# Attention and large-kernel convolution on one core: first statistics blocks ahead of ScalarE's square root, zeros of a mixed operand by GpSimd, first taps of layer 1 loaded in eight pieces

## The chip, the cores and the metric

The kernel runs on one core of one Trainium2 chip. A time is the device time of a whole launch in microseconds (us). A core has five engines, each with its own instruction queue, worked off in order: TensorE (PE, matmuls), VectorE (DVE), ScalarE (ACT), GpSimd (POOL) and SyncE (SP, which only issues DMAs here). DMAs are issued from SP, ACT and POOL; in the profile their queues are q1, q10 and q0.

## The reference, cut to what matters

The input x is 384 channels of 192 by 192 in float32. Each of two layers normalizes its input over 32 groups of channels, computes something from it, and adds the result to its input.

```python
# layer 0: a 1x1 convolution to q, k, v; 2x2 max pooling; a 3x3 depthwise convolution;
# attention over channels in 8 heads of 48 (4 top-k softmaxes, weighted); gelu; repeat 2x2; a 1x1 projection
x = x + _L0_conv_ref(_gn(x), w_qkv, b_qkv, w_dw, b_dw, w_proj, b_proj, temperature, a1, a2, a3, a4)
# layer 1: seven depthwise convolutions (13x13, 5x5, 7x7, 5x5 dilated 2, 3x3 dilated 3, 4, 5),
# each with its batch norm, summed
x = x + _L1_conv_ref(_gn(x), w0, ..., w6, bn0, ..., bn6)
```

```python
def _gn(v, G=32, eps=1e-5):
    g = v.reshape(B_, G, C_ // G, H_, W_)
    m = jnp.mean(g, axis=(2, 3, 4), keepdims=True)
    s = jnp.var(g, axis=(2, 3, 4), keepdims=True)
    return ((g - m) / jnp.sqrt(s + eps)).reshape(v.shape)
```

## The kernel before

The 384 channels are three blocks of 128 partitions (NJ = 3). The work goes through these stages, one after another.

**Statistics of x.** VectorE reads all of x once with bn_stats. The first 16 rows of the image come as four tiles `xt` (1152 KB each, all three channel blocks), which stay in memory and are used again in the next stage. The rest comes as 66 blocks `xs` (one channel block, 1536 columns, 768 KB), with ten tiles in rotation. `load_block` issues the DMA of a block: the first six and all odd ones from ScalarE, the other even ones from SP. VectorE takes the blocks in order, and `rows_stats` takes one xt tile ahead of blocks 0, 1, 3 and 5. On ScalarE, the table load and the square root of the batch norms' variances (`rsqrt`, L85, whose input waits for the load of `bn`) stand ahead of the loads. On SP, the four xt loads and that of the projection weights `wqk` stand ahead of block 6. GpSimd builds the combined 13x13 filter `wf` from the seven filters. The three small parameters bq, wd and bdw of the next stage are loaded from ScalarE.

**q, k and v (L332, about half of the time).** The stage goes over the image in bands of 8 rows, first for q and k, then for v. TensorE multiplies, VectorE pools (L343) and applies the depthwise taps (L379), ScalarE does the rest. Meanwhile GpSimd writes 2x2 sums of the normalized x to memory (`sums`), and Toeplitz bands of the layer-1 filter are written to memory (`zd`). Attention's softmax is computed between the steps. v ends up in memory that stays, as a tile of 128 x 3 x 96 x 96.

**Attention times v (L723).** A loop over 24 groups of 4 pooled rows multiplies the block-diagonal attention matrix `bd` with v. A head crosses from one channel block into the next, so the middle block of outputs also needs part of channel blocks 0 and 2. These parts go together into a mixed operand: `mix` copies them with GpSimd into one of three tiles `hx`, and the weights that belong to them are copied with ScalarE into `bdx`. The other partitions of both must be zero. VectorE writes these zeros at the head of the stage, in program order behind its last depthwise taps. ScalarE applies gelu in place.

**Projection (L1037).** It goes over channel block (i, 3) and group (b, 24), 72 cells n in all. For each cell TensorE multiplies, ScalarE evicts with the bias into a tile `pjs` (three in rotation, L1045) and issues its store to memory (`pd`, L1055), and VectorE adds the matching `sums` (tile `smj`, L1024, loaded from SP four cells ahead) and takes layer 1's statistics (`cell`, L1052, L1053). Between the cells the statistics of a finished channel block are turned into scales (`derive`), and the first two of layer 1's 48 groups of channels are prepared: `load_rows` loads rows of x (`raw`) and of the stored projection (`up`), `load_taps` the taps (`wt`, from `zd`), both from GpSimd; `residual` adds them, `patch` puts a term into the taps, `normalize1` and `arrange` make the patch tile `xp`. All of this is placed by hand at given cells; generators in `running` go on by one step for each cell.

**Layer 1 (L966).** For each of 48 groups of 8 channels, five matmuls for each channel work on taps and patches; loads, residual, normalization and the output run ahead or behind by a group or two. Its memory for later groups comes from what the projection gives back.

The order inside these stages is the program's own (`manual_schedule`). The framework places waits on semaphores: a DMA from SP or ScalarE takes one of eight semaphores in turn and waits for the last one to use it, and GpSimd's DMAs do the same with eight of their own. A tile whose memory another tile held waits for the last user of that one.

Of the kernel before, what the change touches and what calls it, by code (L numbers as in the profile page):

```python
# [14 lines left out]
P = 128  # L15
# [38 lines left out]
def tile_attn_then_large_kernel_conv(ctx: ExitStack, tc: tile.TileContext, a: dict, out: bass.AP):  # L54
# [106 lines left out]
    with (  # L161
        tc.tile_pool(name="s1", bufs=1) as s1,
        tc.tile_pool(name="sx", bufs=10) as sx,
        tc.tile_pool(name="s_ps", bufs=2, space=PSUM) as s_ps,
        tc.manual_schedule(),
    ):

        for B in range(2):
            for sb in range(2):
                load(B, sb)  # L170
        FX = 2 * R * 2 * W
        FB = 1536
        NX = (HW - FX) // FB
        NS0 = 2 * 2 * 2
        stats = s1.tile([P, NJ, NS0 + NX * (FB // 512), 6], F32, name="stats")
        bn = s1.tile([P, NJ, 4, 7], F32, name="bn")
        nc.gpsimd.dma_start(
            out=bn.rearrange("p j q i -> p j (q i)"), in_=a["bn"].rearrange("(j p) s -> p j s", p=P)
        )
        wf = s1.tile([P, NJ, KX, K0], F32, name="wf")  # L180
        nc.gpsimd.memset(wf, 0.0)
        wbs = []
        for i, (k, _) in enumerate(((K0, 1),) + BRANCHES):
            wb = s1.tile([P, NJ, k, k], F32, name=f"wb{i}")
            nc.gpsimd.dma_start(
                out=wb.rearrange("p j a b -> p j (a b)"), in_=a[f"w{i}"].rearrange("(j p) s -> p j s", p=P)
            )
            wbs.append(wb)
        xss = []

        def load_block(n):
            j, b = divmod(n, NX)
            xt = sx.tile([P, FB], F32, name=f"xs_{n}", tag="xs")

            eng = nc.scalar if n < 6 or n % 2 == 1 else nc.sync
            eng.dma_start(out=xt, in_=x[j * P : (j + 1) * P, FX + b * FB : FX + (b + 1) * FB])
            xss.append(xt)

        scale = in_one(rsqrt(s1, bn[:, :, 3, :], 1e-5, "bn"))
        nc.vector.tensor_mul(scale, scale, bn[:, :, 0, :])  # L200
        sh = s1.tile([P, NJ, 7], F32, name="sh")
        nc.vector.tensor_mul(sh, bn[:, :, 2, :], scale)
        nc.vector.tensor_sub(sh, bn[:, :, 1, :], sh)
        nc.vector.tensor_reduce(shift, sh, AX.X, ALU.add)
        for n in range(10):
            load_block(n)
        c0 = BC - 1
        for j in range(NJ):
            nc.gpsimd.tensor_scalar(wf[:, j, c0 : c0 + K0, :], wbs[0][:, j], scale[:, j, 0:1], None, ALU.mult)
            for i, (k, r) in enumerate(BRANCHES):  # L210
                o = PAD - r * (k - 1) // 2
                n = r * (k - 1) + 1
                zv = wf[:, j, c0 + o : c0 + o + n : r, o : o + n : r]
                wb = wbs[i + 1][:, j]
                nc.gpsimd.tensor_scalar(wb, wb, scale[:, j, i + 1 : i + 2], None, ALU.mult)
                nc.gpsimd.tensor_add(zv, zv, wb)

        def rows_stats(n):
            xt = xts[n // 2, n % 2]
            for j in range(NJ):  # L220
                nc.vector.bn_stats(stats[:, j, 2 * n, :], xt[:, j, :512])
                nc.vector.bn_stats(stats[:, j, 2 * n + 1, :], xt[:, j, 512:])

        for n in range(NJ * NX):
            if n in (0, 1, 3, 5):
                rows_stats((n + 1) // 2)
            j, b = divmod(n, NX)
            xt = xss.pop(0)
            for q in range(FB // 512):
                nc.vector.bn_stats(stats[:, j, NS0 + b * (FB // 512) + q, :], xt[:, q * 512 : (q + 1) * 512])  # L230
            if n + 10 < NJ * NX:
                load_block(n + 10)
            if b == NX - 1:
                nc.vector.bn_aggr(mv0[:, j, :], stats[:, j].rearrange("p n s -> p (n s)"))  # L234
        nc.sync.dma_start(
            out=wfd.rearrange("(j p) s -> p j s", p=P), in_=wf.rearrange("p j x y -> p j (x y)")
        )
        nc.vector.tensor_copy(gn0, in_one(group_stats(s1, s_ps, mv0, "g0")))  # L238
# [7 lines left out]
    with ExitStack() as ctx_v:  # L246
# [433 lines left out]
        with (  # L680
# [22 lines left out]

            bdx = b1.tile([P, P], F32, name="bdx")
            with tc.manual_schedule():
                for t in [bdx] + hx:
                    nc.vector.memset(t, 0.0)
                nc.scalar.copy(bdx[P - LO :], bd[P - LO :, 0, P : 2 * P])
                nc.scalar.copy(bdx[:HI], bd[:HI, 2, P : 2 * P])
                sms = [load_sums(b) for b in range(2)]  # L710
                for b in range(2):
                    mix(b)
                for b in range(NBB):
                    if b + 2 < NBB:
                        mix(b + 2)
                    if b + 2 < NBB:
                        sms.append(load_sums(b + 2))
                    pss = {}
                    for i in (0, 2, 1):
                        ps = b1_ps.tile([P, NBK], F32, tag=f"av{i}", name="av")  # L720
                        js = AV_BLOCKS[i]
                        for j in js:
                            nc.tensor.matmul(  # L723
                                ps,
                                lhsT=bd[:, j, i * P : (i + 1) * P] if j < NJ else bdx,
                                rhs=v[:, j, b * RB : (b + 1) * RB, :].rearrange("p r w -> p (r w)")
                                if j < NJ
                                else hx[b % 3],
                                start=(j == js[0]),
                                stop=(j == js[-1]),  # L730
                            )
                        pss[i] = ps
                    for i in (0, 2, 1):
                        nc.scalar.activation(
                            v[:, i, b * RB : (b + 1) * RB, :].rearrange("p r w -> p (r w)"), pss[i], AF.Gelu
                        )
                    sm = sms.pop(0)
                    for j in range(NJ):
                        nc.vector.bn_stats(stats[:, j, b, :], sm[:, j])
# [162 lines left out]
                )  # L902
                yield

        def load_taps(k, eng=nc.sync):
            wt = taps[k] = rotate("wt", k, k, [P, CC, ZS], 3)
            j, kk = divmod(k, KK)
            eng.dma_start(out=wt, in_=zds[j][kk * CC : (kk + 1) * CC].rearrange("c p z -> p c z"))

        def patch(k):  # L910

# [101 lines left out]
        with (  # L1013
# [4 lines left out]
            with tc.manual_schedule():  # L1018
# [9 lines left out]
                for n in range(NJ * NBB):  # L1028
# [7 lines left out]
                    for j in range(NJ):  # L1036
# [4 lines left out]
                            start=(j == 0),  # L1041
                            stop=(j == NJ - 1),
                        )
                    pj = by.tile([P, 2, RB // 2, WS], F32, tag="pjs", name="pjs")
                    nc.scalar.activation(  # L1045
                        pj.rearrange("p y r w -> p r y w"),
                        ps.rearrange("p (r y w) -> p r y w", y=2, w=WS),
# [12 lines left out]
                        ),  # L1060
                        in_=pj.rearrange("p y r w -> p y (r w)"),
                    )
                    if n == NBB + 4:
                        running.append(load_rows(0, nc.gpsimd))
                    if n == NBB + 9:
                        load_taps(0, nc.gpsimd)
                    if n == NBB + 13:
                        running.append(residual(0, nc.vector, 3))
                    if n == NBB + 20:
                        assert not running  # L1070
# [24 lines left out]
    with (  # L1095
        tc.tile_pool(name="l2", bufs=1) as l2,
        tc.tile_pool(name="more", bufs=1) as more,
        tc.tile_pool(name="lo", bufs=2) as lo,
    ):
        pools["more"] = more  # L1100
        with tc.manual_schedule():
            load_taps(1)
            patches(l2, 1)
            all_of(load_rows(2))
            last = None
            for k in range(NK):
                if k + 3 < NK:
                    all_of(load_rows(k + 3))
                if k + 2 < NK:
                    load_taps(k + 2)  # L1110
                    all_of(residual(k + 2))
                co = lo.tile([P, CC, NT, NBQ], F32, tag="co", name=f"co_{k}")
                for c in range(CC):
                    convolve(k, c, co)
                    if c == CC - 2:
                        advance()
                    if c == 0:
                        if k + 1 < NK:
                            all_of(arrange(k + 1))
                            patch(k + 1)  # L1120
                        if last is not None:
                            finish(k - 1, last, lo)

                    n = c - (CC - 3 if k == 0 else 3)
                    if 0 <= n < 3 and k + 2 < NK:
                        normalize1(k + 2, n)
                last = co
            finish(NK - 1, last, lo, 2, (nc.sync, nc.scalar, nc.gpsimd, nc.sync))
# [50 lines left out]
```

## Time and profile before

| What | us |
|---|---|
| median of 3 runs | 3153.32 (3152.84 to 3154.92) |
| profiled execution | 3152.71 |
| its span in the trace | 3150.9 |
| PE busy | 2952.2 (94%) |
| DVE busy | 2506.1 (80%) |
| ACT busy | 1229.4 (39%) |
| POOL busy | 896.7 (28%) |

The span is what the trace covers; 1.8 us of the profiled execution lie around it. Times inside the trace are counted from the span's start. In it, the statistics end at 158, attention times v begins at 1950, the projection at 2053 and layer 1 at 2214. A busy share is an average over all stages and says nothing about who sets the pace in one of them; for that the chain of waits is used, which goes back from the last instruction from each step to what released it.

### The profile page before, as it was taken

How to read it: one execution, taken by the hardware profiler on the slowest of the kernel's cores; microseconds unless marked ns; L12 is line 12 of the kernel's file. 1: busy time of each engine (PE TensorE's matmuls, PEld its weight loads, DVE VectorE, ACT ScalarE, POOL GpSimd, SP SyncE). 2: the span in 40 equal slices, each digit the busy share in tenths (PEclk: the TensorE clock that was granted, in tenths of full speed). 3: DMA queues.
4: the chain of work that ended last, by engine and by line, in shares of the span. 5: the costliest groups of instructions: out<-in, count | busy, mean ns of one | idle time of the engine just before them, and what ended most of it. 6: DMA issues, size and time to landing. Idle time of an engine off the chain costs nothing.

```text
span 3150.9 us, 31869 instructions
## 1 busy us (share of the span) xinstructions
PE 2952.2 (94%) x10906; PEld 1962.4 (62%) x10906; DVE 2506.1 (80%) x3407; ACT 1229.4 (39%) x2290; POOL 896.7 (28%) x1071
## 2 busy tenths in 40 slices
PE   0099999999999999999999999999999999999998
PEld 0056666666666666665555555555777777777776
DVE  7968787878788787879999898457788777777775
ACT  0034444444444444444444543322333333333332
POOL 3033231323323232312222222200333333333331
PEclk9999999999999999999999999999999999999999
DMA  9933442424243342423333332476999999999994
GB/s 386 369 110 98 130 126 98 153 76 152 86 138 109 119 141 87 151 90 99 119 107 99 116 113 79 149 213 195 244 266 242 239 244 245 248 247 246 248 219 116
DMA packets 275154, 528.67 MB, mean 168 GB/s; under 512 B 22290, under 2 KB 189664, under 8 KB 274992
## 3 DMA queue, kind: packets, MB, share of 16 engines
q1 hardware_dynamic: 203632, 332.49, 39.1%
q0 software_dynamic: 44896, 151.32, 16.0%
q10 hardware_dynamic: 26464, 42.82, 3.7%
q8 instruction: 87, 1.43, 0.2%
q14 instruction: 75, 0.61, 0.1%
HBM read 365.18 MB, written 161.37 MB: 167 GB/s over the span
## 4 chain that ended last, share of the span: by engine, by line
PE 86%; DVE 9%; DMA 3%; issue 1%; ACT 0%; POOL 0%; ACTq 0%; DVEq 0%; POOLq 0%
PE qkv L332 49%; PE conv L966 28%; DVE stats L230 3%; DVE v L379 3%; PE pj L1037 3%; PE av L723 3%; PE gram L420 2%; PE tr L408 2%; DMA xs<-in_x 1%; DMA pd<-pjs 1%; DVE mx L343 1%; DMA up<-pd 0%; DVE cell L1052 0%; DVE mv L234 0%; ACT pjs L1045 0%
## 5 line engine op out<-in xcount | busy, mean ns | idle before, releaser
L332 PE MATMUL qkv<-xt,wqk 128*128 128x384 f32 x3456 | 1132.5, 487 | 1.3 <-ACT xt L309 1.3
L966 PE MATMUL conv<-xp,wt 128*128 128x288 f32 (+1 forms) x3840 | 919.4, 403 | 2.4 <-ACT co L974 2.4
L332 PEld LDWEIGHTS qkv<-xt,wqk 128*128 128x128 f32 x3456 | 650.2, 190 | 435.6 <-ACT xt L309 2.1
L966 PEld LDWEIGHTS conv<-xp,wt 128*128 128x128 f32 x3840 | 730.1, 190 | 189.3 <-ACT co L974 2.8
L379 DVE SCALAR_TENSOR_TENSOR acc<-pooled,wd,acc 128x384 f32<-128x384 f32 (+2 forms) x1152 | 732.3, 636 | 30.6
L343 DVE TENSOR_REDUCE mx<-qkv 128x192 f32<-128x768 f32 x432 | 412.5, 955 | 243.2 <-PE qkv L332 230.9
L948 DVE STREAM_TRANSPOSE xp<-xn 128x4608 f32<-128x4608 f32 (+1 forms) x107 | 441.9, 4130 | 182.7 <-PE conv L966 162.7
L350 ACT ACTIVATE pooled<-mx,bq 128x192 f32<-128x192 f32 x432 | 196.8, 456 | 963.0 <-DVE mx L343 962.6
L332 PE MATMUL qkv<-xt,wv 128*128 128x384 f32 x1728 | 563.4, 487 | 1.6 <-ACT xt L309 1.1
L332 PEld LDWEIGHTS qkv<-xt,wv 128*128 128x128 f32 x1728 | 325.6, 190 | 234.4 <-ACT xt L309 7.1
L974 ACT ACTIVATE co<-conv,cb 128x288 f32<-128x288 f32 x384 | 191.7, 499 | 593.6 <-PE conv L966 593.6
L317 POOL TENSOR_TENSOR sum<-xt 128x192 f32<-128x192 f32 x144 | 96.9, 673 | 1117.6 <-ACT xt L309 1116.2
L379 DVE SCALAR_TENSOR_TENSOR v<-pooled,wd,v 128x384 f32<-128x384 f32 (+2 forms) x576 | 375.6, 652 | 15.2
L309 ACT ACTIVATE xt<-xt,gn 128x768 f32<-128x768 f32 x288 | 285.2, 1014 | 2.9 <-DVE gn L238 2.9
L991 POOL DMA_DIRECT2D out<-o x191 | 106.1, 586 | 572.2 <-DVE o L982 522.2
L925 POOL TENSOR_TENSOR raw<-raw,up 128x2496 f32<-128x2496 f32 x46 | 231.1, 5025 | 23.1 <-DMA raw<-in_x 18.2
L982 DVE STREAM_TRANSPOSE o<-co 128x2304 f32<-128x2304 f32 (+1 forms) x50 | 209.7, 4196 | 19.8 <-ACT co L974 19.8
L102 PE MATMUL g_ps<-mv,gm 128*32 128x1 f32 x18 | 1.8, 185 | 158.4 <-DVE mv L234 157.8
L1037 PE MATMUL pj<-v,wp 128*128 128x384 f32 x432 | 145.3, 495 | 2.7 <-DVE cell L1052 2.2
L230 DVE BATCH_NORM_STATS2 stats<-xs 128x6 f32<-128x512 f32 x198 | 118.0, 679 | 10.3 <-DMA xs<-in_x 10.3
L1037 PEld LDWEIGHTS pj<-v,wp 128*128 128x128 f32 x432 | 82.1, 193 | 59.1 <-DVE cell L1052 3.3
L318 POOL TENSOR_TENSOR sum<-sum,xt 128x192 f32<-128x192 f32 x144 | 113.2, 786 | 11.3
(170 smaller groups left out, 1725.0 us busy)
## 6 DMA issues: line engine op xcount, KB each, us to landing
xt<-in_x SPq DMA_DIRECT2D x96, 1152.0 KB, 7.1
wt<-zd SPq DMA_DIRECT2D x47, 1536.0 KB, 13.2
raw<-in_x SPq DMA_DIRECT2D x182, 312.0 KB, 13.3
out<-o POOLq DMA_DIRECT2D x188, 288.0 KB, 7.1
zd<-v POOLq DMA_DIRECT2D x96, 416.0 KB, 4.6
up<-pd SPq DMA_DIRECT2D x184, 156.0 KB, 12.4
xs<-in_x ACTq DMA_DIRECT2D x36, 768.0 KB, 9.3
xs<-in_x SPq DMA_DIRECT2D x30, 768.0 KB, 11.9
```

Source lines behind the costliest of these rows:

```text
L230: nc.vector.bn_stats(stats[:, j, NS0 + b * (FB // 512) + q, :], xt[:, q * 512 : (q + 1) * 512])
L309: nc.scalar.activation(xt[:, j], xt[:, j], AF.Identity, bias=gn0[:, j, 1:2], scale=gn0[:, j, 0:1])
L332: nc.tensor.matmul(ps[:, r, : 2 * W], lhsT=wq[:, j, mm * P : (mm + 1) * P], rhs=xt[:, j, r * 2 * W : (r + 1) * 2 * W], start=(j == 0), sto ...
L343: nc.vector.tensor_reduce(mx, ps[:, :, : 2 * W].rearrange("p r (y w x) -> p r w y x", y=2, x=2), AX.XY, ALU.max,)
L350: nc.scalar.activation(pool_t[m][:, k : k + SR, 1 : 1 + WS], mx, AF.Identity, bias=bq[:, m : m + 1])
L379: nc.vector.scalar_tensor_tensor(acc[:, :nt], pool_t[m][:, k0 + dy : k0 + dy + nt, dx : dx + WS], wd[:, m, t : t + 1], acc[:, :nt], ALU.mu ...
L925: eng.tensor_add(rv, rv, uv.unsqueeze(2).to_broadcast([P, (m1 - m0) * WS, 2]))
L948: nc.vector.transpose(bass.AP(at.tensor, at.offset, [list(at.ap[0]), [NBQ, n], [1, NBQ], [NQ * NBQ, CC], [ME * NBQ, NE]],), bass.AP(row.te ...
L966: nc.tensor.matmul(ps[:, t0:t1], lhsT=wt[:, c, o : o + P], rhs=d[:, c, g + 2 * t0 : g + 2 * t1 - 1 : 2, :], start=(g == 1), stop=(g == NGR ...
L974: nc.scalar.activation(co[:, c], ps, AF.Identity, bias=cb[:, cc : cc + 1])
L982: nc.vector.transpose(bass.AP(at.tensor, at.offset, [list(at.ap[0]), [2 * W, n], [BC, NBQ], [W, 2], [1, BC]]), bass.AP(of.tensor, of.offse ...
L1037: nc.tensor.matmul(ps, lhsT=wp[:, j, i * P : (i + 1) * P], rhs=v[:, j, b * RB : (b + 1) * RB, :].rearrange("p r w -> p (r w)"), start=(j = ...
```

## The change

Blocks 0 and 1 are issued from ScalarE before its square root, and blocks 6 and 7 by ScalarE. VectorE takes an xt tile ahead of blocks 1, 3, 5 and 7. The zeros of bdx and hx are written by GpSimd, each hx tile's right ahead of the first copies into it. The taps of group 0 are loaded in eight DMAs, one for each channel, as a generator that is started at cell 24 (NBB); rows and residual of group 0 are placed a few cells later. pjs has six tiles. The other calls of load_taps run the generator to its end at once, with one DMA as before.

```diff
-            eng = nc.scalar if n < 6 or n % 2 == 1 else nc.sync
+            eng = nc.scalar if n < 8 or n % 2 == 1 else nc.sync
...
+        for n in range(2):
+            load_block(n)
         scale = in_one(rsqrt(s1, bn[:, :, 3, :], 1e-5, "bn"))
...
-        for n in range(10):
+        for n in range(2, 10):
             load_block(n)
...
         for n in range(NJ * NX):
-            if n in (0, 1, 3, 5):
-                rows_stats((n + 1) // 2)
+            if n in (1, 3, 5, 7):
+                rows_stats(n // 2)
...
-                for t in [bdx] + hx:
-                    nc.vector.memset(t, 0.0)
+                nc.gpsimd.memset(bdx, 0.0)
                 nc.scalar.copy(bdx[P - LO :], bd[P - LO :, 0, P : 2 * P])
                 nc.scalar.copy(bdx[:HI], bd[:HI, 2, P : 2 * P])
                 sms = [load_sums(b) for b in range(2)]
-                for b in range(2):
-                    mix(b)
+                for b in range(3):
+                    nc.gpsimd.memset(hx[b], 0.0)
+                    if b < 2:
+                        mix(b)
...
-        def load_taps(k, eng=nc.sync):
+        def load_taps(k, eng=nc.sync, n=CC):
             wt = taps[k] = rotate("wt", k, k, [P, CC, ZS], 3)
             j, kk = divmod(k, KK)
-            eng.dma_start(out=wt, in_=zds[j][kk * CC : (kk + 1) * CC].rearrange("c p z -> p c z"))
+            for c in range(0, CC, n):
+                c0 = kk * CC + c
+                eng.dma_start(out=wt[:, c : c + n], in_=zds[j][c0 : c0 + n].rearrange("c p z -> p c z"))
+                yield
...
-                    pj = by.tile([P, 2, RB // 2, WS], F32, tag="pjs", name="pjs")
+                    pj = by.tile([P, 2, RB // 2, WS], F32, tag="pjs", name="pjs", bufs=6)
...
-                    if n == NBB + 4:
+                    if n == NBB + 8:
                         running.append(load_rows(0, nc.gpsimd))
-                    if n == NBB + 9:
-                        load_taps(0, nc.gpsimd)
-                    if n == NBB + 13:
+                    if n == NBB:
+                        running.append(load_taps(0, nc.gpsimd, 1))
+                    if n == NBB + 14:
                         running.append(residual(0, nc.vector, 3))
...
-            load_taps(1)
+            all_of(load_taps(1))
...
-                    load_taps(k + 2)
+                    all_of(load_taps(k + 2))
```

## The prediction

> **What bounds the kernel now.** I read the page first: PE is busy 94% of the span, the chain that ended last is 86% PE, so a change off TensorE pays only where that chain leaves PE. Then I asked for the chain in order of time. It leaves PE in three places for more than a few us, and the change touches all three. First place, the statistics stage (columns: start us, length us, what):
>
> ```profile
> 5.55 12.32 DMA xs<-in_x
> 17.89 26.95 DMA xs<-in_x
> 44.86 28.59 DVE stats L230 x48
> ```
>
> The second load is block 6, the first statistics block on SP's queue: issued at 17.89, landed at 44.8. VectorE's timeline shows what that costs, and the windows (engine busy times, then PE clock, DMA share, GB/s) what runs out at the stage's end:
>
> ```profile
> 44.86 15.52 DVE L230 BATCH_NORM_STATS2 stats<-xs 128x6 f32<-128x512 f32 x26 [7.24 <-DMA xs<-in_x]
> ```
>
> ```profile
> 135.00:145.00 10.00, 0.00 (x0) 0.00 (x0) 10.00 (x18) 0.00 (x0) 0.00 (x0) 1.00 1.02 418
> 145.00:150.00 5.00, 0.00 (x0) 0.00 (x0) 5.00 (x9) 0.00 (x0) 0.00 (x0) 1.00 0.74 287
> 150.00:155.00 5.00, 0.00 (x0) 0.00 (x0) 5.00 (x10) 0.00 (x0) 0.00 (x0) 1.00 0.00 1
> ```
>
> After 44.86 VectorE never stops until 158.26; the DMAs are full until about 148.7 and then done. So VectorE sets the end, 9.6 us behind the DMAs, and only its idle time before 44.86 can be won.
>
> The other two places, from the same chain later on:
>
> ```profile
> 1957.08 0.63 DVE v L379
> ...
> 1957.80 0.17 DVE bdx L707
> ...
> 1959.62 92.52 PE av L723 x278
> ...
> 2108.15 11.84 DMA pd<-pjs
> ...
> 2158.99 12.63 DMA pd<-pjs
> ```
>
> At 1957 PE waits for the mixed operand, whose zeros stand on VectorE behind the last taps. At 2108 and 2159 ScalarE, which evicts the projection (pjs), waits for stores of earlier evictions to land. The DMA view of 2100 to 2126 says why (packets, MB, share of 16 engines; then KB each and us to landing):
>
> ```profile
> q0 software_dynamic: 864, 3.17, 42.7%
> q1 hardware_dynamic: 1291, 1.76, 23.3%
> q10 hardware_dynamic: 2448, 1.77, 22.2%
> ...
> wt<-zd POOLq DMA_DIRECT2D x1, 1536.0 KB, 15.1
> ```
>
> GpSimd's queue (q0) brings rows and taps of layer 1 while stores (q10) and sums (q1) go on. A quiet and a disturbed window:
>
> ```profile
> 2060.00:2070.00 10.00, 10.00 (x33) 5.89 (x32) 6.16 (x12) 2.90 (x5) 0.00 (x0) 1.00 0.68 203
> ...
> 2120.00:2125.00 5.00, 2.04 (x5) 1.42 (x6) 2.73 (x11) 1.45 (x3) 0.00 (x0) 0.69 0.69 241
> ```
>
> The steady stage needs 203 GB/s at a DMA share of 0.68; in the disturbed one PE works 2.04 of 5 us and its clock falls to 0.69.
>
> **What the Trainium skill says.** "DMA: Bandwidth & Descriptors", section "Queues, rings and completion order": each DMA engine goes round the queues that have work, one whole packet at a time. The trace agrees: from 10 to 15 us ScalarE's queue moved 170 packets and SP's 166, though the former's are twice as large. "TensorE: Matmul & The Clock Gate", section "What's actually happening": an idle window of about 3.4 us drops the clock. The trace agrees in kind: after 4.9 us idle before 2123 the clock was 0.69 and 0.63, after gaps up to 2.2 us near 2170 it stayed 1.00. "SBUF — State Buffer", section "SBUF: two separate sides": a VectorE operation with two SBUF inputs locks GpSimd out only of operations that read SBUF; a memset reads none, so the taps should not stretch it. No run here shows that.
>
> **Part 1, statistics.** Blocks 0 and 1 are issued on ScalarE before its table load and square root; blocks 6 and 7 both go by ScalarE, so the first block on SP is 8. bq, wd and bdw, first on ScalarE before, move in the built program behind block 15; four pooled memsets move up on POOL. VectorE takes one xs block ahead of each of the four xt tiles.
> SP's ring still carries four xt (1152 KB), wqk and then one block; turns being equal per packet, block 8 lands where block 6 did, near 44.8. By then VectorE has two blocks more behind it. A block is 39.12/22 = 1.78 us, so 3.56 us. Against it: at that time ScalarE's ring has carried one more block (786 KB at 418 GB/s = 1.9 us), for it the bulk starts some 1.5 us earlier, because 0 and 1 don't wait for bn (landed at 4.86) and its square root. Net -0.4; I take **3.2 us**. Later the DMA floor (148.7 + one block 1.8 + aggregate 2.2 = 152.7) lies under VectorE's new end (155.1), so nothing takes it back. wd's 1152 packets of 36 bytes take about 11 ns each (1074 packets, 36.6% of 16 engines in 2 us), 0.8 us of all 16: covered by the backlog. If block 8 lands late or the moved small loads hold up block 17, it is 0; if the stage ends on the DMA floor, 5.5.
>
> **Part 2, zeros.** Four VectorE memsets leave, four on POOL come, each just ahead of its copies. In the built program POOL's bdx memset still waits for VectorE's last tap (the space was a pooled tile), so the gap at 1953 to 1959.6 stays. Chain before: taps end 1957.71, bdx 0.17, hx 0.38, copies from 1958.51. On POOL, from its memsets (78 elements 0.16, 588 elements 0.60), bdx 0.21 and hx 0.43: copies from about 1958.5. **0**, between -0.3 and +0.3. hx1 and hx2 come 0.4 us and 0.9 us later but are needed only at 1966 and 1970.
> POOL's queue changes: the eight 192 KB pieces of the first taps now stand right behind xn's memset (1948.7), ahead of raw's first two DMAs and of bdx. Eight issues at 0.56 (the 96 KB sums store) 4.5, a memset 0.26, raw 1.18: POOL is through at 1954.7, if raw's waits for the landing of pieces 1 and 2 (it reuses their semaphores) don't bind: these have 4.7 us, and a 288 KB load at 1949 landed in 4.0. Slack to 1957.71: about 3 us. Their 1.57 MB meet DMAs with a share of 0.27.
>
> **Part 3, projection.** Taps leave the burst at 2102: q0 carries 1.60 MB there, not 3.17. pjs has 6 tiles, not 3. Rows(0) moves from n=NBB+4 to +8, but POOL waits for data only (the stores of channel block 0, at 2102.3), so its issue doesn't move; residual(0) moves one cell later, beside PE's matmuls.
> From the rows above a packet costs 206 ns on q0, 75 on q1, 38 on q10. With all three loaded a round is 319 ns, in which stores get 723 bytes per engine, 36 GB/s, where a cell (192 KB in 1.93 us) needs 102: they fall behind by 0.64 of the time. Rows(0), half of the 864 packets, take 8.6 us and put them 5.5 behind; with the taps, 17.2 and 11. Cover before: three tiles less a landing, 3 x 1.93 - 2.0 = 3.8. After: each store also waits for the fourth before it (eight lanes shared with the sums), so eviction n waits for store n-5: 7.7.
> Burst 1: ScalarE's 14 cells from 2101.38 to 2139.03 took 37.65 us against 27.1, so 10.5 lost; 2.4 of it are the statistics matmuls, 8.2 the stall, with 2.6 of slow clock in it (18 matmuls 8.65, later 6.07). After: 5.5 is under 7.7, no stall. I take 7.5, as some waits for VectorE stay.
> Burst 2 (rows(1), 1.92 MB, 10.4 us, 6.6 behind): three cells from 2158.38 took 13.33, so 7.5 lost and 1.7 won back. 6.6 is under 7.7, but VectorE is busy 9.58 of 10 us from 2180 and will hold part back: I take 4 of 5.8.
> Sum **11.5**, between 6 (burst 2 and the clock not won) and 14 (all). Layer 1 starts when the projection releases its memory and is PE bound; it shifts whole.
>
> **Sum.** 3.2 + 0 + 11.5 = 14.7. The profiled execution took 3152.71 (span 3150.9, 1.8 around it), 0.6 below the median of 3153.32. On the median: **3138.6**.
>
> **Rivals.**
> A. The stall moves: stores no longer block ScalarE, but sums or VectorE's order do. For it: VectorE's load after 2180; a sums load shares lanes with the stores. Against: PE leads in the quiet windows, VectorE at 6.2 of 10. Gain 3.2 + 4: 3146.
> B. The zeros come early (POOL doesn't wait for the taps): the gap of 6.6 and its slow clock (2.7) go too: 3129.3. Against: the wait in the built program.
> C. Slower: POOL, in order, is held among the eight pieces until each has landed, so bdx and hx come late. Price 8 x 4.0 = 32 from 1949, 23 past the taps' end: 3161.6. It costs from 1957.7 on and decides above 14.7. Against: four raw and four up stood in flight together at 2102 to 2108.
> D. Part 1 does nothing since the DMAs were full anyway: 3141.8. Against: 9.6 us of VectorE after the last DMA.
>
> **How the numbers follow.** Forecast with D 0.80, A 0.12, B 0.04, C 0.04. A measurement tells some 0.2%, 6.3 us, from no change. Faster: 0.80 + 0.04 + 0.05 of A = 0.89; same 0.07; slower 0.04. The unknowns (part 1: 0 to 5.5, part 3: 6 to 14) and most of A give gains of 6.3 to 19.8, rounded out: 3133 to 3147.
>
> **What would show it.** Right: block 8 as the last wait for xs, near 45, and the statistics ending near 155; copies to hx still from 1958.5 (less the 3 us shift); no wt in GpSimd's queue after 2100, no wait of pjs for pd near burst 1, the clock 1.00 there, the projection 150 us long and not 161. Wrong: POOL idle before bdx for a wt landing; an idle VectorE between 50 and 70 waiting for block 17; ScalarE waiting as long for PE or VectorE as it did for stores.

## The result, and the profile after

| | before | after |
|---|---|---|
| median, us | 3153.18 (4 runs, 3152.84 to 3154.92) | 3136.34 (4 runs, 3135.59 to 3137.03) |
| span of the profiled execution | 3150.9 | 3134.9 |

The ratio is 0.9945, with a 95% interval from 0.9928 to 0.9963: 16.8 us faster, where the forecast said 14.7. The chain of waits in order of time (start us, length us, what), after:

```profile
2.75 21.01 DMA xt<-in_x
24.80 23.10 DMA xs<-in_x
47.92 21.47 DVE stats L232 x36
...
152.04 2.17 DVE mv L236
```

VectorE's timeline at its last wait for a block, and the windows at the stage's end (busy times of PE, its weight loads, VectorE, ScalarE and GpSimd, then PE clock, DMA share, GB/s):

```profile
44.16 25.22 DVE L232 BATCH_NORM_STATS2 stats<-xs 128x6 f32<-128x512 f32 x42 [1.92 <-DMA xs<-in_x]
```

```profile
140.00:145.00 5.00, 0.00 (x0) 0.00 (x0) 5.00 (x10) 0.00 (x0) 0.00 (x0) 1.00 1.01 414
145.00:150.00 5.00, 0.00 (x0) 0.00 (x0) 5.00 (x9) 0.00 (x0) 0.00 (x0) 1.00 0.79 305
150.00:155.00 5.00, 0.51 (x4) 0.42 (x4) 4.31 (x6) 0.00 (x0) 0.00 (x0) 1.00 0.01 3
```

The last wait ends at the same moment as before (44.16, it was 44.86), but it is 1.92 long and not 7.24, because VectorE had more blocks to work on. The stage ends at 152.04 + 2.17 = 154.21, 4.05 earlier. The DMAs still run out before 150, so VectorE is still what sets the end.

At the change to attention times v the chain of waits, asked for that stretch alone, reads as before, with GpSimd in the place of VectorE:

```profile
1954.44 0.02 POOLq L708
...
1954.52 0.20 POOL bdx L708
1954.73 0.37 POOL hx L713
...
1956.29 6.13 PE av L726 x9
```

GpSimd's timeline there shows the eight pieces of taps and what ended the wait after them:

```profile
1945.53 2.14 POOL L913 DMA_DIRECT2D wt<-zd  x4
1948.67 2.12 POOL L913 DMA_DIRECT2D wt<-zd  x4 [0.99 <-issue]
...
1950.97 1.18 POOL L891 DMA_DIRECT2D raw<-in_x  x2
1954.52 0.20 POOL L708 MEMSET bdx<- 128x128 f32 x1 [2.37 <-DVE v L381]
```

GpSimd is through at 1952.15 and waits 2.37 for VectorE's last tap. In the projection the chain now stays on PE through burst 1, the loads of rows from about 2100 on, where it had gone through a store of 12 us (from the chain of the whole run):

```profile
2049.76 50.58 PE pj L1043 x156
2100.49 4.07 PE pj L1043 x12
2104.86 4.07 PE pj L1043 x12
2109.08 6.00 PE pj L1043 x18
2115.39 6.00 PE pj L1043 x18
```

In burst 2 it goes through no store either, but from 2159 to 2178 it is mostly on VectorE. The DMA view of burst 1, from 2097 to 2123 (queue, packets, MB, share of 16 engines), and the window that answers to the disturbed one of before:

```profile
q10 hardware_dynamic: 3286, 2.38, 29.6%
q0 software_dynamic: 496, 1.60, 28.5%
```

```profile
2117.00:2122.00 5.00, 5.00 (x18) 3.07 (x17) 3.34 (x12) 1.73 (x3) 0.00 (x0) 1.00 0.80 239
```

GpSimd's queue carries 1.60 MB there and no taps; PE is busy 5.00 of 5 us, with 18 matmuls and the full clock, where it had done 5 matmuls in 2.04 us at 0.69. The projection takes 149.5 us from the start of its first matmul to the end of its last, and took 161.3.

### The profile page after: what moved, and what is told of

It reads as the page before. It is cut to its first block, busy times and chain, and to the rows that moved or that the text cites. A ratio compares the mean times of both kernels' runs of the same rounds, so it can differ in the third digit from the quotient of the medians.

```text
span 3134.9 us, 31872 instructions
## 1 busy us (share of the span) xinstructions
PE 2948.4 (94%) x10906; PEld 1960.7 (63%) x10906; DVE 2505.6 (80%) x3403; ACT 1229.3 (39%) x2290; POOL 901.3 (29%) x1082
## 4 chain that ended last, share of the span: by engine, by line
PE 87%; DVE 9%; DMA 2%; issue 1%; ACT 0%; SPq 0%; POOL 0%; DVEq 0%; POOLq 0%; ACTq 0%
PE qkv L334 49%; PE conv L972 28%; PE pj L1043 4%; DVE v L381 3%; DVE stats L232 3%; PE av L726 3%; PE gram L422 2%; PE tr L410 2%; DVE mx L345 1%; DMA xs<-in_x 1%; DMA xt<-in_x 1%; DMA raw<-in_x 1%; DVE stats_t L1059 0%; DVE cell L1058 0%; DVE mv L236 0%
```

## The experiments

Four points of each trace make the table. "Stretch 1" is from the projection's first matmul to the first matmul of `shp` (in `patches`), and holds burst 1; "stretch 2" is from there to the first of the second group of `shp` matmuls, and holds burst 2. The ratio is to the kernel before, run beside it on the same chip.

| kernel | median us | ratio (95%) | statistics end | first hx matmul | stretch 1 | stretch 2 |
|---|---|---|---|---|---|---|
| before | 3153.18 | | 158.26 | 1959.62 | 83.7 | 57.1 |
| changed | 3136.34 | 0.9945 (0.9928 to 0.9963) | 154.21 | 1956.29 | 75.9 | 53.2 |
| changed, again | 3135.77 | 0.9952 (0.9936 to 0.9968) | 154.72 | 1956.61 | 75.9 | 54.2 |
| part 1 alone | 3147.87 | 0.9987 (0.9980 to 0.9994) | 154.13 | 1956.52 | 81.1 | 56.8 |
| part 2 alone | 3153.16 | 1.0003 (0.9994 to 1.0012) | 158.18 | 1960.04 | 84.1 | 56.7 |
| six tiles alone | 3141.06 | 0.9967 (0.9954 to 0.9980) | 158.38 | 1960.54 | 76.9 | 52.8 |
| early taps alone | 3150.76 | 0.9995 (0.9987 to 1.0004) | 157.38 | 1959.53 | 80.8 | 57.3 |
| changed, taps late | 3137.48 | 0.9955 (0.9940 to 0.9970) | 154.35 | 1956.03 | 75.9 | 53.1 |
| changed, taps in one DMA | 3135.52 | 0.9950 (0.9936 to 0.9965) | 154.37 | 1956.38 | 75.9 | 53.3 |
| changed, five tiles | 3136.83 | 0.9953 (0.9938 to 0.9968) | 154.05 | 1956.59 | 75.9 | 53.2 |
| changed, four tiles | 3139.72 | 0.9962 (0.9950 to 0.9975) | 154.01 | 1955.70 | 77.0 | 56.2 |
| changed, blocks 0 and 1 behind the root | 3134.96 | 0.9948 (0.9930 to 0.9966) | 153.70 | 1955.10 | 75.9 | 53.6 |
| changed, zeros early | 3127.97 | 0.9928 (0.9910 to 0.9946) | 154.42 | 1950.09 | 75.9 | 52.8 |
| only what pays | 3127.76 | 0.9923 (0.9907 to 0.9940) | 153.34 | 1948.19 | 77.2 | 53.7 |

### The changed kernel again

> The changed kernel itself again, beside the others on the same chip. Theory: 3136.3 within 1.5, statistics end near 154.2, gap before the first hx matmul 6.5, projection 149.5 within 0.7. The first matmuls of layer 1 after its gap of 2.4: the clock 1.00 as in the first trace if the gap is always too short to lower it, 0.66 as in the kernel before if it is chance; that is worth 1.7.

The median, the statistics and the gap are as expected. The projection, 150.6 long, misses its 149.5 within 0.7, all of it in stretch 2, which is 1.0 longer: ScalarE waited 4.2 for a store in it, and VectorE 5.0 for loads of sums, where it had waited 2.9. So burst 2 is not covered to the last with six tiles. The 50 matmuls took 12.19 again.

### Part 1 alone

The kernel before, with

```diff
-            eng = nc.scalar if n < 6 or n % 2 == 1 else nc.sync
+            eng = nc.scalar if n < 8 or n % 2 == 1 else nc.sync
...
+        for n in range(2):
+            load_block(n)
         scale = in_one(rsqrt(s1, bn[:, :, 3, :], 1e-5, "bn"))
...
-        for n in range(10):
+        for n in range(2, 10):
             load_block(n)
...
-            if n in (0, 1, 3, 5):
-                rows_stats((n + 1) // 2)
+            if n in (1, 3, 5, 7):
+                rows_stats(n // 2)
```

> The kernel before with part 1 alone (blocks 0 and 1 ahead of the square root, blocks 6 and 7 from ScalarE, xt tiles ahead of blocks 1, 3, 5, 7). Theory (VectorE sets the end of the stage, so what it does before the last wait for xs is won whole and kept): last wait for xs ends near 44.2 instead of 44.86, statistics end near 154.2 instead of 158.26, attention times v starts 3.3 to 4.1 earlier, time 3149.2 to 3150. The start of layer 1 shows the same shift and no more, since the projection keeps its 161. Rival (the stage's gain comes only together with another part, or is given back in the q, k, v stage): 3153.

The statistics end at 154.13, and the median lies 4.1 under that of the kernel before beside it (3152.0). The gain of the stage is whole, needs no other part and is given back nowhere. The expected 3149.2 to 3150 were counted from 3153.2; beside this kernel the one before ran in 3152.0. The trace is of the fastest of this kernel's 17 runs (3143.7, where the median is 3147.87), and its projection took 158.5, though nothing in it was changed and 161 had been expected; so its stretch 1 of 81.1 is no measure of what a median run does.

### Blocks 0 and 1 behind the square root

The changed kernel, with

```diff
-        for n in range(2):
-            load_block(n)
         scale = in_one(rsqrt(s1, bn[:, :, 3, :], 1e-5, "bn"))
...
-        for n in range(2, 10):
+        for n in range(10):
             load_block(n)
```

> The changed kernel with blocks 0 and 1 back behind ScalarE's square root; blocks 6 and 7 still go by ScalarE and the xt tiles still come ahead of blocks 1, 3, 5, 7. Theory (the two blocks that VectorE has behind it at the last wait make the gain, the early issue only some of it): last wait for xs ends between 44.2 and 45.7, statistics end between 154.2 and 155.7, time 3136.5 to 3138. Rival (the early issue makes the gain): last wait and end as in the kernel before, near 158, time 3140.

VectorE's timeline in this kernel, its first work and its last wait for a block:

```profile
4.90 0.18 DVE L83 TENSOR_SCALAR bn_ve<-bn 128x21 f32<-128x21 f32 x1 [4.02 <-DMA bn<-in_bn]
...
42.00 26.28 DVE L230 BATCH_NORM_STATS2 stats<-xs 128x6 f32<-128x512 f32 x42 [1.59 <-DMA xs<-in_x]
```

The timeline of the changed kernel begins otherwise:

```profile
8.15 0.18 DVE L83 TENSOR_SCALAR bn_ve<-bn 128x21 f32<-128x21 f32 x1 [7.27 <-DMA bn<-in_bn]
```

The two loads ahead of the root make the small bn load 3.3 later (7.6 to 8.2 in all eight traces that have them, 4.7 to 5.2 in the six others). The statistics end a little earlier without them, 153.70, and the last wait ends at 42.00. So the early issue brings nothing. The gain is that of the other edit: blocks 6 and 7 come by ScalarE's queue, and the xt tiles stand one or two blocks later in VectorE's order. These two were not tried apart.

### Part 2 alone

```diff
-                for t in [bdx] + hx:
-                    nc.vector.memset(t, 0.0)
+                nc.gpsimd.memset(bdx, 0.0)
...
-                for b in range(2):
-                    mix(b)
+                for b in range(3):
+                    nc.gpsimd.memset(hx[b], 0.0)
+                    if b < 2:
+                        mix(b)
```

> The kernel before with part 2 alone (zeros of bdx and hx by GpSimd). Theory: bdx's zeros still begin when VectorE's last tap has ended (1957.7), so the first matmul on hx stays at 1959.6 within 0.3 and the time is 3153.2 within 0.5. Rival B (zeros come early): hx matmul about 6 earlier and the clock kept, 3144. Rival (GpSimd's memsets are dearer than VectorE's on the path): 0.5 to 1 slower.

PE waits 6.53 ahead of its first hx matmul and waited 6.56; the median is the same. The 0.4 by which that matmul is later arose before the last taps, in the q, k, v stage, and comes in other kernels too.

### Zeros early

The changed kernel, with bdx and two hx tiles in the place of wv, in a pool that nothing but wv used:

```diff
+        aq = ctx_a.enter_context(tc.tile_pool(name="aq", bufs=1))
...
-        wv = a2.tile([P, NJ, C], F32, name="wv")
+        wv = aq.tile([P, NJ, C], F32, name="wv")
...
+        b3 = ctx_v.enter_context(tc.tile_pool(name="b3", bufs=1))
+        bdx = b3.tile([P, P], F32, name="bdx")
+        hx = [b3.tile([P, NBK], F32, name=f"hx{n}") for n in range(2)]
...
-            hx = [b1.tile([P, NBK], F32, name=f"hx{n}") for n in range(3)]
+            hx.append(b1.tile([P, NBK], F32, name="hx2"))
...
-            bdx = b1.tile([P, P], F32, name="bdx")
```

> The changed kernel, with bdx and two of the three hx tiles in memory that held only wv before (wv has a pool of its own, bdx and hx0, hx1 take its place when it closes), so that their zeros wait for the last matmul of the q, k, v stage and not for VectorE's last tap; order of the code unchanged. Theory (the wait for the last tap is all that keeps the gap of 6.5 and the slow clock after it): the first hx matmul within 2 of the last matmul on v that precedes it, clock 1.00 in the stage, attention times v 6 to 9 earlier at its end, time 3127 to 3130. Rival 1 (hx2, still behind the taps, or ScalarE's table load and copies hold PE next): gain 2 to 5, 3131.5 to 3134. Rival 2 (PE only waits later for the same taps or for gelu): no gain, 3136.3.

PE's timeline, first of the changed kernel at the gap, then of this one:

```profile
1956.29 1.65 PE L726 MATMUL av<-hx,bdx 128*128 128x384 f32 x2 [6.53 <-POOL hx L702]
```

```profile
1946.76 3.49 PE L729 MATMUL av<-v,bd 128*128 128x384 f32 x10 [1.05 <-DVE mx L346]
1950.09 0.81 PE L729 MATMUL av<-hx,bdx 128*128 128x384 f32 x2
1950.73 3.39 PE L729 MATMUL av<-v,bd 128*128 128x384 f32 x10
1953.95 0.81 PE L729 MATMUL av<-hx,bdx 128*128 128x384 f32 x2
```

and the windows over the same stretch, first of the changed kernel, then of this one:

```profile
1953.00:1956.00 3.00, 0.00 (x0) 0.00 (x0) 2.49 (x7) 1.21 (x3) 1.35 (x4) 0.50 0.50 123
1956.00:1962.00 6.00, 5.71 (x9) 3.20 (x10) 1.90 (x4) 2.52 (x5) 3.95 (x9) 0.50 1.01 364
```

```profile
1953.00:1956.00 3.00, 3.00 (x11) 1.81 (x10) 2.83 (x6) 0.98 (x2) 1.90 (x4) 1.00 0.86 261
1956.00:1962.00 6.00, 5.74 (x19) 3.14 (x18) 0.74 (x4) 2.13 (x5) 4.96 (x10) 1.00 1.03 278
```

The gap is gone and the clock with it: in the 6 us from 1956, 19 matmuls and not 9. The projection starts 8.8 earlier (2041.01, it was 2049.76), and the median is 7.8 under that of the changed kernel run again beside it (3135.77). So the forecast's case B had nearly the right price (9.3 under the forecast) for a change that this one does not make: to have GpSimd write the zeros is worth nothing by itself, and to free their memory earlier on top of that is worth 8. Early memory with the zeros left to VectorE was not tried; there they would still stand behind its last taps in program order. The third tile, still behind the last tap, costs a wait of 0.26.

### Six tiles alone, and early taps alone

The kernel before with `bufs=6` for pjs and nothing else:

> The kernel before with six pjs tiles and nothing else; the taps still load in one DMA at 2102. Forecast's theory (stores fall 11 us behind in burst 1 against a cover of 7.7, 6.6 in burst 2): some 3.3 of burst 1's stall stays, burst 2 gains about 4; projection 152 to 155 instead of 161.1, time 3144 to 3147. Rival R1 (only the taps' bandwidth matters): burst 1 as before, projection 157, time 3149. Rival R2 (tiles alone do it all): projection 149.5 to 150, time 3141.5.

The kernel before with the new `load_taps`, three pjs tiles, and

```diff
-                    if n == NBB + 4:
+                    if n == NBB + 8:
                         running.append(load_rows(0, nc.gpsimd))
-                    if n == NBB + 9:
-                        load_taps(0, nc.gpsimd)
-                    if n == NBB + 13:
+                    if n == NBB:
+                        running.append(load_taps(0, nc.gpsimd, 1))
+                    if n == NBB + 14:
                         running.append(residual(0, nc.vector, 3))
```

> The kernel before with the first taps in eight pieces at cell 24, rows and residual at their later cells, and three pjs tiles as before. Forecast's theory (burst 1 puts the stores 5.5 behind against a cover of 3.8; burst 2 untouched): 1.7 of stall stays in burst 1, which gains about 6.5 with its clock; projection 154 to 155.5, time 3146 to 3147.5. Rival R1 (taps are all of burst 1): no stall in burst 1, gain 8, projection 153. Rival R2 (place of the taps is worth nothing, tiles do it all): projection 161, time 3153.

The tiles alone bring 6.8 in stretch 1 and 4.3 in stretch 2, 11.1 of the 11.8 that the projection gained in all: rival R2. With the early taps alone the projection took 158.6, where the forecast's theory had 154 to 155.5. They bring 2.9 in stretch 1 against the trace of before and 0.3 against that of part 1 alone, which has the projection of before but lies 4 us under its own median; their median is 1.2 under before's, within what can be told from nothing. In the chain of waits of this kernel the store of burst 1 is still there:

```profile
2106.54 9.61 DMA pd<-pjs
...
2156.46 12.78 DMA pd<-pjs
```

The DMA view from 2108 to 2112 shows that rows alone hold stores up, in the kernel with early taps,

```profile
q0 software_dynamic: 212, 0.73, 88.1%
q1 hardware_dynamic: 130, 0.18, 18.7%
q10 hardware_dynamic: 23, 0.02, 1.7%
```

and in the kernel before from 2116 to 2120, when the last loads of rows land (at 2118.02) and the taps are under way:

```profile
q0 software_dynamic: 234, 1.06, 68.5%
q1 hardware_dynamic: 230, 0.31, 21.6%
q10 hardware_dynamic: 235, 0.17, 13.1%
```

In the first, stores get 23 packets, 0.02 MB in 4 us, where a store of 192 KB leaves every 1.93 us; in the second they get 0.17 MB, though q0 moves more. The rows come first in the kernel before too: from 2106 to 2110 stores got 0.04 MB there. So to move the taps away leaves the worst of the burst where it was. From 2104 to 2112 the stores moved 0.20 of the 0.81 MB that 8 us bring, so they were some 6.0 us behind that steady need. In the kernel before the shortage lasts until 2120: 0.66 of 1.63 MB in 16 us, some 9.5 behind.

### Taps late, or in one DMA, on top of the whole change

The changed kernel with `load_taps(0)` in one DMA at NBB + 9, and rows and residual at NBB + 4 and NBB + 13:

> The changed kernel with the first taps put back: one DMA at cell NBB + 9, rows and residual at NBB + 4 and NBB + 13. Theory T2 (formed from the tiles-alone run, projection 150.2, and the taps-alone run, 158.6 beside 158.5 to 161.3 in kernels that left the projection alone: six tiles cover both bursts with the taps in or out): projection 150 to 150.7, layer 1 at most 0.7 later than in the changed kernel, time 3136.3 to 3137.5. Rival (the forecast's: the burst with taps puts stores 11 behind, over a cover of 7.7): projection 153 or more, time 3139.5 or more.

The changed kernel with

```diff
-                        running.append(load_taps(0, nc.gpsimd, 1))
+                        running.append(load_taps(0, nc.gpsimd))
```

> The changed kernel with the first taps at the same place, cell NBB, but in one DMA. Theory T2 (neither place nor pieces matter, their transfer meets free bandwidth at 1945 to 1956): GpSimd through with its issues some 3.4 earlier, but bdx's zeros still behind the last tap; gap before the first hx matmul 6.5, projection 149.5 to 150.2, time 3136.3 within 1. Rival (one DMA of 1.57 MB holds up the first sums, or wp, where pieces leave room between): attention times v later by 1 or more.

Both give 75.9 and 53.1 or 53.3, the changed kernel's own numbers. In one DMA or eight, early or late, and with rows and residual four and one cells earlier, the taps cost nothing here once there are six tiles. Late taps may cost up to 1.3 elsewhere: 76.9 with six tiles alone, 77.2 in the last experiment, beside 75.9 in each of the six traces with early taps and five or six tiles.

### Five tiles, four tiles

The changed kernel with `bufs=5`:

> The changed kernel with five pjs tiles. Theory (each store also waits, by its semaphore, for the fourth store before it, so eviction n waits for store n-5 at the latest; a sixth tile is never used ahead): as with six, projection 149.5 to 150.2, time within 1 of 3136.3. Rival (each tile counts for 1.93 of cover): projection 151 or more, time 3138 or more.

The changed kernel with `bufs=4`:

> The changed kernel with four pjs tiles, cover 4 x 1.93 less 2.0 = 5.7. The forecast's sizes (rows alone put the stores 5.5 behind in burst 1 and 6.6 in burst 2): burst 1 as with six, burst 2 loses 0.9; projection 150 to 150.5, time 3137. Theory T2 (a store lands 9.6 after its issue in burst 1 even without the taps, so 7.6 behind, and 12 in burst 2): PE loses up to 1.9 in each burst; projection 152 to 153.5, time 3139 to 3140.

Five are as good as six in both stretches, as the wait for the fourth store before would have it. With four, stretch 1 loses 1.1 and stretch 2 loses 3.0, most of the 4.0 that the tiles had brought there; neither set of sizes had them so unequal. ScalarE's waits from 2130 to 2185 with four tiles, and with five (total us, times, longest):

```profile
ACT pjs L1051 <- DMA pd<-pjs: 7.4, 3, 5.6
```

```profile
ACT pjs L1051 <- DMA pd<-pjs: 1.0, 1, 1.0
```

One tile more takes 6.4 of waiting away, more than the 1.93 that a tile holds. That a count of tiles times 1.93 says how much burst is covered was not shown.

### Only what pays

The kernel before with the `n < 8` rule and the later xt tiles of part 1 (blocks 0 and 1 behind the root), six tiles, and part 2 with the memory of the early zeros; taps, rows and residual as before:

> The kernel before with only what the runs so far showed to pay: blocks 6 and 7 by ScalarE and the xt tiles ahead of blocks 1, 3, 5, 7, but blocks 0 and 1 behind the square root as before; six pjs tiles; bdx, hx0 and hx1 in wv's place with their zeros by GpSimd. The first taps stay one late DMA. Theory (the early issue and the taps' place carry nothing): statistics end near 153.7, projection 149.2 to 150.2, time 3126.5 to 3128.5, as with the early zeros on top of the whole change (3127.97) or a little under it. Rival (with the gap closed, the late taps cost again, GpSimd's copies and the taps no longer being apart): projection 151 or more, 3129.5 or more.

3127.76 is the same as with the early zeros on top of the whole change, within the intervals. The rival was right on the projection (151.3 long, with 77.2 in stretch 1), but an earlier end of the statistics (153.34) and no gap at all before the hx matmuls made it good. Both kernels beat the changed one by 8 us. The two together, early taps and blocks 0 and 1 behind the root, were not tried.

## Why the prediction was right

The parts of the sum, with spans after against before, in us:

| step | predicted | measured |
|---|---|---|
| part 1, statistics end | -3.2 | -4.05 |
| q, k, v, up to that wait | 0 | +0.75 |
| part 2, wait ahead of the hx matmul | 0 | -0.03 |
| attention times v | 0 | +0.4 |
| part 3, projection | -11.5 | -11.8 (stretch 1 -7.8, stretch 2 -4.0) |
| layer 1, through the 50 matmuls named below | 0 | -1.6 |
| remainder | 0 | +0.3 |
| sum | -14.7 | -16.0 |

**Part 1.** The mechanism held: the first SP block lands where it did, VectorE has two blocks more behind it, nothing takes it back. The term of -0.4, for ScalarE's longer ring against the earlier issue, had the wrong sign: block 8 landed 0.7 before the time of block 6. But the reason that was given for an earlier bulk, blocks 0 and 1 ahead of the root, is not it; without it, the last wait ended earlier still, at 42.00.

**Part 2.** Right in its cause, and shown by the kernel that removes it: bdx's zeros wait for VectorE's last tap because of their memory. What was not seen is that this could be undone for 8 us. GpSimd's slack was 2.37 and not 3, since the eight issues took 5.3, with a pause of 0.99 in them that no view explains.

**Part 3.** Both bursts came out as sized, 7.8 for 7.5 and 4.0 for 4, and in burst 2 VectorE did take over as the part held back. But the mechanism was told in an order that gave the credit wrongly. "Taps leave the burst" stood first, and rows alone were to put the stores 5.5 behind, with the taps 11. Those two backlogs were about right (6.0 and 9.5). What failed is what was to follow from them, once they were tested apart: with three tiles a backlog of 6.0, less a cover of 3.8, should have left some 2 of stall, but ScalarE waits 5.3 for one store and PE stops for so long that the clock falls (0.86 and 0.80 in the 10 us from 2119 of the kernel with early taps), so that most of the loss stays; with six, 9.5 costs 1.3 at most. The tiles are the step that carries 11.1 of the 11.8.

**Rivals.** A (the stall moves) is out in burst 1: ScalarE waits for a store once, for 2.0, and PE goes on. B (the zeros come early) is out for this change: the wait of 6.53 stayed. C (GpSimd held at each piece) is out: all eight were issued within 5.3 us. D (part 1 does nothing) is out by part 1 alone.

**What was not in the sum.** 1.7 of the 16.0 came from layer 1. Its first 50 matmuls after a short wait took 13.88 in the kernel before and 12.19 after. That is the PE clock, in a place that the change doesn't touch, and it goes either way (last section). Without it the spans differ by 14.3, with 14.7 predicted. That they come so near is in part luck. Part 1 gave 0.9 more than its term, and q, k, v and attention times v took 1.1 back: the way from the end of the statistics to the wait is 1801.4 to 1802.6 in the 12 traces that have the wait, and shortest in that of before, for no reason that a run shows. And stretch 1 of before isn't steady: with three tiles and late taps it took 83.7, 84.1 and, with part 1 alone, 81.1.

**The clock.** The prediction read its own trace as keeping the clock at 1.00 after gaps up to 2.2. The same trace has it at 0.66 in the 5 us after a gap of 2.35, at 2240.20, which it leaves out; that is where layer 1's 1.7 comes from.

## What to carry to other kernels

When an evicting engine waits for its stores, look first at how many tiles it may leave unstored, and only then for a better moment for the other transfers: more tiles took away what moving 1.5 MB out of the burst did not. Where a memset waits, ask what it waits for before asking which engine should do it; the engine alone made no difference, and another pool for the memory on top of it was worth 8 us, about a third of them by the clock that the gap had cost. A change of several edits whose sum comes out right says nothing of each: here two of the edits, blocks 6 and 7 with the later xt tiles, and the six tiles, carried nearly all of it.

## What the runs showed of the hardware

**The clock after a wait of 2 us goes either way.** Ahead of the same 50 matmuls PE waits 2.0 to 2.7 us in every kernel. The same line of PE's timeline, of the changed kernel and of the one with five tiles:

```profile
2225.56 12.19 PE L972 MATMUL conv<-xp,wt 128*128 128x288 f32 x50 [2.41 <-ACT co L980]
```

```profile
2224.73 13.88 PE L972 MATMUL conv<-xp,wt 128*128 128x288 f32 x50 [2.61 <-ACT co L980]
```

The granted clock in the first 5 us is 1.00 in the first and 0.66 in the second. In 4 of 14 traces the 50 matmuls took 13.88, after waits of 2.19, 2.35, 2.45 and 2.61; in the other ten 12.19, after waits of 2.03 to 2.65. The length of the wait doesn't decide it. The Trainium skill, "TensorE: Matmul & The Clock Gate", section "What's actually happening", says that the activity window is free-running and doesn't start with the work; that the same gap can then fall either way would follow from it, and the traces fit, but none shows the window. Where the section has the clock fall after an idle window of about 3.4 us, as the prediction cites it, these traces differ: it fell after 2.19 to 2.61. The clock also goes both ways in attention times v with its gap of 6.5: two of the traces have it 1.4 shorter than most (91.4 and 91.5, not 92.5 to 92.9), and in them the clock from 2 to 4 us after the gap is 0.76 and 0.70, where the changed kernel has 0.50. A single trace is uncertain by such steps of 1.4 to 1.7, and so a comparison of two is worth no more than that until each stage has been compared by itself.

**Queues do not always get equal turns.** In the 4 us of the early-taps kernel shown above, q0 moved 212 packets and q10 23, though a store was outstanding all the while (the one issued at 2106.54 landed 9.61 later). The prediction drew on the skill's page "DMA: Bandwidth & Descriptors" for one packet each in turn. The kernel before has just that from 2116 to 2120 (234, 230 and 235), and not from 2106 to 2110, in the rows, the taps being issued only at 2108.20: 206 on q0, 145 on q1, 63 on q10. What makes the difference was not found; nor does a run show that what the trace counts as packets (272 for one store) are the packets that the page means. Over a whole burst equal turns still sized the stores' delay about right; within it stores can get next to nothing for 4 us.

**A small load is late behind large ones on other queues.** bn is 42 KB on GpSimd's queue. With two blocks of 768 KB started ahead of the root on ScalarE's queue it came 3 us later, as the two VectorE lines above show (4.90 and 8.15).
